# First attention: outputs kept by channel and divided by way of DMA and GpSimd, maxima turned by VectorE in 32x32 blocks

## The chip, the core and the metric

The kernel runs on one core of a Trainium2 chip, in one launch. The core has a matrix engine (TensorE, PE in the profile; its weight loads are listed apart as PEld), VectorE (DVE), ScalarE (ACT), GpSimd (POOL), and SyncE (SP), which here only issues DMAs. Each engine works through its own queue in order and waits on semaphores. The metric is the device time of one execution in microseconds (us).

## The reference

A residual stream `x` of 1024 tokens by 512 channels in float32 passes through four sublayers, each behind a LayerNorm without weights: a first attention with 32 heads of 16 channels, a feed-forward with a router and low-rank experts, a second attention with 32 heads of 128 channels, and the feed-forward again. Only the first attention and the start of the feed-forward behind it are touched here:

```python
    def attention_fwd(x, wq, wk, wv, wo, n_heads=32):
        B, T, C = x.shape
        hd = C // n_heads
        xq = (x @ wq.T).reshape(B, T, n_heads, hd)
        xk = (x @ wk.T).reshape(B, T, n_heads, hd)
        xv = (x @ wv.T).reshape(B, T, n_heads, hd)
        xq = rotary_pos_emb(xq)
        xk = rotary_pos_emb(xk)
        scale = hd ** (-0.5)
        scores = jnp.einsum('bqhd,bkhd->bhqk', xq, xk) * scale
        causal = jnp.tril(jnp.ones((T, T), dtype=bool))
        scores = jnp.where(causal[None, None], scores, NEG_INF)
        probs = jax.nn.softmax(scores.astype(jnp.float32), axis=-1).astype(xq.dtype)
        out = jnp.einsum('bhqk,bkhd->bqhd', probs, xv).reshape(B, T, C)
        return out @ wo.T
...
    x = x + _L0_attn_a_ref(_layernorm(x, axis=-1), L0_attn_a_wq, L0_attn_a_wk, L0_attn_a_wv, L0_attn_a_wo)
```

## The kernel before

**Chunks.** The 32 heads are taken four at a time, in 8 chunks `c` (`NCA`). A head has 16 channels and is padded to 32 rows (`PADA`), so a chunk fills the 128 partitions. `qT` and `kT` hold queries and keys with channels on partitions. The first padding row of each head, row `j * PADA + DA`, is one in `kT`, and in `qT` it first holds zero and later the negated maximum of each query's scores.

**Two passes of scores.** The scores of a chunk are made twice. `row_scores` (L304, matmul at L310) has queries on partitions, and `maxima` (L319, VectorE at L327 and L330) reduces them to a negated maximum per query and head, in `neg`: 128 queries on partitions, 4 heads by 4 tiles along the free side, for each half of the 1024 queries. `with_maxima` (L341) brings them into the padding row of `qT`: a transpose on TensorE (`tp_m`, L345), a copy by ScalarE (`negT`, L347) and four DMAs on SP, one per head (L350). Then `col_scores` (L355, matmul at L362) makes the scores again with keys on partitions, now with the maximum already subtracted, adds the causal mask by a matmul (L380), and `exponentials` (L382) takes their exponential.

**The product.** `product` (L384, matmul at L396) multiplies the exponentials with values into `oT`, with channels on partitions and 512 queries (`QC`) along the free side. A column of ones in the values makes the seventeenth row of each head the sum of the exponentials. ScalarE copies `oT` out of PSUM (`oTs`, L407).

**Normalization.** `normalize` (L410) turns `oTs` back to queries on partitions by four transposes on TensorE (`tp_o`, L99), copies 17 columns per head (`os`, L417), takes the reciprocal of the sums on VectorE (`rsa`, L419), and multiplies on GpSimd (L421) into `o`, which has queries on partitions and 512 channels along the free side.

**Steps.** `step(rc, cc, n)` (L440) does one of 10 steps `n` of the column work of chunk `cc` and of the row work of chunk `rc = cc + 1`, in two halves of two heads each: score matmuls of both interleaved, then maxima, exponentials, what is due, and half a product of two steps earlier. The column heads of the first half are 2 and 3. Steps 0 to 2 of the columns read the first half of the queries and steps 3 to 9 the second; the rows finish the first half of the queries within steps 0 to 2, the second in step 9. Work for later is put in `later` and run in the next step, behind the exponentials of its first half: `with_maxima(rc, 0)` in step 5, `with_maxima(cc, 1)` in step 1, the two normalizations of a chunk in step 5 and in step 2 of the next chunk.

**Order.** The code is written in an order, and a scheduler at build time follows it but lets an instruction go ahead on its engine where an earlier one isn't ready by its plan. [...]

**After the attention.** The output projection needs channels on partitions, so `gather` (L1013) transposes each tile of 128 queries again (`tp_ao`), with a copy by VectorE (`aoT`, L1016), and `out_projection` (L1019, L1022) multiplies with `wo` and adds to `x` (L1023). Two tiles are done in `tail` (L1025), with the last normalization between them; the other six in the first turns of the feed-forward (`projected`, L1042), beside its LayerNorm, whose power runs on GpSimd (L93). SP's next work is to load the weights of the second attention (L669, L671).

Of the kernel before, what the change touches and what calls it, by code (L numbers as in the profile page):

```python
# [9 lines left out]
F32 = mybir.dt.float32  # L10
BF16 = mybir.dt.bfloat16
AF = mybir.ActivationFunctionType
ALU = mybir.AluOpType
# [3 lines left out]
P = 128  # L17
T = 1024
NT = T // P
C = 512  # L20
KC = C // P
QC = 512
# [7 lines left out]
DA = C // HA  # L30
PADA = 32
# [7 lines left out]
B = 32  # L39
# [25 lines left out]
class Block:  # L65
# [174 lines left out]
    def attend_a(self, ctx_pool, pt, work, ps_s, ps_o, qT, kT, v_p, project_qk, project_v, midway, tail):  # L240
        nc, tc = self.nc, self.tc
        HC = P // PADA
        with ExitStack() as ctx:
            cp = ctx.enter_context(tc.tile_pool(name="a_c", bufs=1))
            qk = ctx.enter_context(tc.tile_pool(name="a_qk", bufs=2))
            o_sb = []

            next(project_qk)

# [26 lines left out]
            def neg(c, half):  # L276

                if (c, half) not in negs:
                    negs[c, half] = qk.tile([P, HC, NT // 2], F32, tag="neg", name=f"neg{c}_{half}", bufs=3)
                return negs[c, half]  # L280
# [59 lines left out]

            def with_maxima(c, half):  # L341

                rows = HC * NT // 2
                ps = ps_s.tile([P, QC], F32, tag="s", name=f"tp_m{c}{half}")[:rows, :P]
                nc.tensor.transpose(ps, neg(c, half).rearrange("p h i -> p (h i)"), self.ident)  # L345
                t = qk.tile([P, P], F32, tag="negT", name=f"negT{c}_{half}")[:rows, :]
                nc.scalar.copy(t, ps)  # L347
                for j in range(HC):
                    row = j * PADA + DA
                    nc.sync.dma_start(  # L350
                        qT[row : row + 1, c, half * QC : (half + 1) * QC].rearrange("o (i t) -> o i t", t=P),
                        t[j * NT // 2 : (j + 1) * NT // 2, :],
                    )

            def col_scores(c, n, heads, made):  # L355

# [27 lines left out]
            def product(c, n, p):  # L384

                first, last = n in (0, 3), n in (2, NP - 1)
                pieces = col_pieces(n)
                qc, middle = pieces[0][0], pieces[-1][-1] // 2
                if first:
                    outs[c, qc] = ps_o.tile([P, QC], F32, tag="o", name=f"oT{c}_{qc}")  # L390
                o = outs[c, qc]
                for lo, hi in ((0, middle), (middle, 2 * middle)):
                    for _, b, at, end in pieces:
                        x0, x1 = max(lo, at), min(hi, end)
                        for j in range(HC if x0 < x1 else 0):
                            nc.tensor.matmul(  # L396
                                o[rows_of(j), QC - end + x0 : QC - end + x1],
                                lhsT=v_cols(b, c * HC + j),
                                rhs=p[:, j, x0:x1],
                                start=first and x0 == 0,  # L400
                                stop=last and x1 == 2 * middle,
                            )
                    yield
                if not last:
                    return
                oT = work.tile([P, QC], F32, tag="w", name=f"oTs{c}_{qc}")
                nc.scalar.copy(oT, o)  # L407
                later.append(lambda: normalize(c, qc, oT))

            def normalize(c, qc, oT):  # L410
                if not o_sb:
                    o = ctx_pool.tile([P, NT, C], F32, tag="o", name="o")
                    o_sb.extend(o[:, i] for i in range(NT))
                ps = self.transpose4(ps_s, [oT[:, i * P : (i + 1) * P] for i in range(4)], f"o{c}{qc}", tag="s")
                pv = ps.rearrange("p a (h d) -> p a h d", d=PADA)
                os = qk.tile([P, 4, HC, DA + 1], F32, tag="os", name=f"os{c}_{qc}")
                nc.scalar.copy(os, pv[:, :, :, : DA + 1])  # L417
                rs = qk.tile([P, 4, HC], F32, tag="rs", name=f"rsa{c}_{qc}")
                nc.vector.reciprocal(rs, os[:, :, :, DA])  # L419
                for a in range(4):  # L420
                    nc.gpsimd.tensor_tensor(  # L421
                        o_sb[qc * 4 + a][:, c * HC * DA : (c + 1) * HC * DA].rearrange("p (h d) -> p h d", d=DA),
                        os[:, a, :, :DA],
                        rs[:, a, :].unsqueeze(2).to_broadcast([P, HC, DA]),
                        ALU.mult,
                    )

            def drain(gens):
                gens = list(gens)
                while gens:  # L430
                    for g in list(gens):
                        try:
                            next(g)
                        except StopIteration:
                            gens.remove(g)

            later = []
            pending = []

            def step(rc, cc, n):  # L440


                p, made, madeT = None, {}, {}
                due = list(later)
                later.clear()
                if cc is not None:
                    p = pt.tile([P, HC, QC], F32, tag="p", name=f"p{cc}_{n}")
                    pending.append((cc, n, p))
                turns = product(*pending.pop(0)) if len(pending) > 2 else iter(())
                both = rc is not None and cc is not None  # L450
                for half in range(2 if both else 1):
                    rows, cols = (2 * half, 2 * half + 1), (2 - 2 * half, 3 - 2 * half)
                    if not both:
                        rows = cols = range(HC)
                    gens = []
                    if cc is not None:
                        gens.append(col_scores(cc, n, cols, madeT))
                    if rc is not None:
                        gens.append(row_scores(rc, n, rows, made))
                    drain(gens)  # L460
                    if rc is not None:
                        maxima(rc, n, rows, made)
                    if cc is not None:
                        exponentials(n, cols, madeT, p)
                    while due:
                        due.pop(0)()
                    next(turns, None)
                drain([turns])
                if rc is not None and n == 4:
                    later.append(lambda: with_maxima(rc, 0))  # L470
                if cc is not None and n == 0:
                    later.append(lambda: with_maxima(cc, 1))


            for i in range(1, NT):
# [8 lines left out]
            for c in range(NCA):  # L484
                if c == NCA // 2:
                    midway()
                for n in range(NP):
                    step(c + 1 if c + 1 < NCA else None, c, n)
            for item in pending:
                drain([product(*item)])  # L490
            tail(o_sb, ps_s, work, later)
        return o_sb

# [490 lines left out]
def hybrid_block_kernel(  # L986
# [20 lines left out]
    nc = tc.nc  # L1007
    blk = Block(ctx, tc, x)

    ao = ctx.enter_context(tc.tile_pool(name="a_out", bufs=1))  # L1010
    wo = ao.tile([P, KC, C], F32, tag="wo", name="a_wo")

    def gather(o, i, work, tp, wtag, tag):  # L1013
        ps = blk.transpose4(tp, [o[i][:, k * P : (k + 1) * P] for k in range(KC)], f"ao{i}", tag)
        oT = work.tile([P, KC * P], F32, tag=wtag, name=f"aoT{i}").rearrange("p (k t) -> p k t", t=P)
        nc.vector.tensor_copy(oT, ps)  # L1016
        return oT

    def out_projection(i, oT, ps_m, tag):  # L1019
        pm = ps_m.tile([P, C], F32, tag=tag, name=f"pm_ao{i}")  # L1020
        for kc in range(KC):
            nc.tensor.matmul(pm, lhsT=oT[:, kc, :], rhs=wo[:, kc, :], start=(kc == 0), stop=(kc == KC - 1))  # L1022
        nc.vector.tensor_add(blk.x[i], blk.x[i], pm)  # L1023

    def tail(o, ps, work, later):  # L1025
        oTs = [gather(o, i, work, ps, "w", "s") for i in range(2)]
        out_projection(0, oTs[0], ps, "s")
        while later:
            later.pop(0)()
        out_projection(1, oTs[1], ps, "s")  # L1030

    weights = [w_baseT, w_rhT, lora_B, b_base]
    f_ctx = ExitStack()
# [8 lines left out]
    def projected(work, tp, ps_m):  # L1042
        yield
        yield
        oT = gather(o, 2, work, tp, "oT", "tp")
        for i in range(2, NT):
            nxt = gather(o, i + 1, work, tp, "oT", "tp") if i + 1 < NT else None
            out_projection(i, oT, ps_m, "pm")
            oT = nxt
            yield  # L1050

    xnT, xn = [], []
# [1 line left out]
    def normalize(i, tp):  # L1054
        if not xnT:
            xnT.append(ao.tile([P, KC, T], F32, tag="o", name="xnTb"))
            xn.append(ao.tile([P, KC, C], F32, tag="wo", name="xnb"))
        blk.normalized(i, xn[0][:, i % KC, :], "b")
        if i > 1:
            channels(i - 2, tp)  # L1060
# [77 lines left out]
```

## Time and profile before

| what | value |
|---|---|
| median of 3 runs | 1655.16 us (1654.3 to 1655.9) |
| the profiled execution's own time | 1654.29 us |
| its span on the core | 1652.2 us |
| granted TensorE clock | 1.00 |
| first attention, steps with columns | about 119 to 401 us of the span |
| `tp_o` transposes | 64 of 286 ns |
| `tp_m` transposes | 16 of 273 ns |
| `tp_ao` transposes | 32 of 276 ns |
| copies by ScalarE: `oTs`, `os`, `negT` | 16 of 592, 16 of 393, 16 of 244 ns |
| copies by VectorE: `aoT` | 8 of 686 ns |
| multiplies by GpSimd in `normalize` | 64 of 293 ns |
| DMAs of maxima on SP | 64 of 2 KB |

The page gives each engine's busy time and its share of the span. Groups of instructions are listed by line, engine and operation, with what is written and read (`out<-in`), the number of instructions, busy time and the mean of one. A line can be that of a helper: all transposes by TensorE have L99 except `tp_m`. The order of time lists start, duration, engine and line of single instructions, merged where they are alike; a bracket holds the idle time before an instruction and what ended it. For SP, the duration is the time in which the queue is held by issuing the DMA, not the time of the transfer.

### The profile page before, as it was taken

The page shows a single profiled execution, that of the slowest core. Times are in us where ns is not written, and L with a number is a line of the kernel's source. Part 1 is how long each engine was busy: PE and PEld are TensorE (multiplying, and loading weights), DVE is VectorE, ACT ScalarE, POOL GpSimd, SP SyncE. Part 2 cuts the span into 40 slices and gives each one's busy share as a digit, 9 for nine tenths or more (in the row PEclk, how much of TensorE's full clock was granted, in tenths as well). Part 3 has the DMA queues.
Part 4 walks back from the last instruction along what each step waited for, and adds up shares of the span by engine and source line. Part 5 has one row for each costly group of instructions (what it writes and reads, how often), then busy time and mean ns, then how long its engine had stood idle before and what let it go on. Part 6 is the DMA issues. An engine that isn't in the chain of part 4 may idle for free.

```text
span 1652.2 us, 31905 instructions
## 1 busy us (share of the span) xinstructions
PE 1632.8 (99%) x12920; PEld 937.4 (57%) x12920; DVE 1100.7 (67%) x2832; ACT 555.2 (34%) x1230; POOL 351.6 (21%) x524
## 2 busy tenths in 40 slices
PE   9999999999999999999999999999999999999998
PEld 5544444444654657556655765655665576556654
DVE  4557777771553886776677677677667767777762
ACT  2325565555212333233233223223323322332230
POOL 3000000001311332223213222222322222222140
PEclk9999999999999999999999999999999999999999
DMA  5000000001003200200200120020020012000001
GB/s 198 1 1 2 3 2 2 2 2 40 1 27 88 65 1 27 65 27 26 65 27 7 51 60 2 27 65 26 27 65 26 16 45 64 1 27 27 2 1 51
DMA packets 60866, 52.03 MB, mean 31 GB/s; under 512 B 5744, under 2 KB 47472, under 8 KB 60720
## 3 DMA queue, kind: packets, MB, share of 16 engines
q1 hardware_dynamic: 59408, 46.06, 9.7%
q0 software_dynamic: 784, 2.90, 0.5%
q8 instruction: 101, 1.65, 0.4%
q10 hardware_dynamic: 528, 1.05, 0.2%
q14 instruction: 45, 0.37, 0.1%
HBM read 30.98 MB, written 2.10 MB: 20 GB/s over the span
## 4 chain that ended last, share of the span: by engine, by line
PE 95%; DVE 3%; ACT 1%; POOL 1%; issue 0%; ACTq 0%; DVEq 0%; POOLq 0%
PE s L798 15%; PE pq L752 13%; PE o L842 13%; PE wo L649 12%; PE sT L362 8%; PE kv L707 7%; PE oT L396 5%; PE pm_f L606 3%; PE or L842 3%; PE s L310 2%; PE pj_v L185 2%; PE pj_q L185 2%; PE pj_k L185 2%; PE sT L380 1%; PE pm_ao L1022 1%; PE st L778 1%
## 5 line engine op out<-in xcount | busy, mean ns | idle before, releaser
L807 ACT ACTIVATE p<-p,nm 128x1024 f32<-128x1024 f32 (+7 forms) x256 | 198.2, 774 | 405.3 <-DVE nm L805 363.6
L810 POOL TENSOR_SCALAR p<-p,rs 128x1024 f32<-128x1024 f32 (+7 forms) x256 | 190.9, 747 | 644.8 <-DVE rs L809 620.9
L798 PE MATMUL s<-kT,qT 128*128 128x512 f32 (+3 forms) x768 | 296.0, 493 | 1.9 <-DVE p L800 1.8
L825 DVE STREAM_TRANSPOSE pT<-p 128x640 f32<-128x640 f32 (+4 forms) x256 | 169.0, 670 | 128.6 <-PE o L842 84.5
L752 PE MATMUL pq<-xnTb,wq 128*128 128x512 f32 x512 | 243.0, 597 | 0.0
L649 PE MATMUL wo<-wo,oT 128*128 128x512 f32 x512 | 240.7, 593 | 1.8 <-DVE nm L805 1.8
L800 DVE SCALAR_TENSOR_TENSOR p<-s,rq,rel 128x512 f32<-128x512 f32 (+3 forms) x384 | 223.9, 601 | 24.6 <-PE s L798 23.4
L798 PEld LDWEIGHTS s<-kT,qT 128*128 128x128 f32 x768 | 140.8, 190 | 164.8 <-issue 117.7
L842 PEld LDWEIGHTS o<-pT,va 32*128 32x128 f32 x5248 | 210.7, 185 | 25.5 <-issue 17.9
L842 PE MATMUL o<-pT,va 32*128 32x256 f32 (+5 forms) x5248 | 220.0, 321 | 0.0
L382 ACT ACTIVATE p<-sT 128x512 f32<-128x512 f32 (+1 forms) x320 | 159.2, 554 | 107.1 <-PE sT L380 67.6
L804 DVE TENSOR_REDUCE nm<-p 128x1 f32<-128x1024 f32 (+7 forms) x256 | 188.7, 738 | 2.9
L310 PE MATMUL s<-kT,qT 32*128 32x512 f32 (+3 forms) x768 | 169.6, 524 | 0.0
L362 PE MATMUL sT<-qT,kT 32*128 32x512 f32 (+3 forms) x768 | 160.5, 524 | 0.0
L649 PEld LDWEIGHTS wo<-wo,oT 128*128 128x128 f32 x512 | 94.6, 190 | 89.0 <-issue 76.3
L752 PEld LDWEIGHTS pq<-xnTb,wq 128*128 128x128 f32 x512 | 92.4, 190 | 88.8 <-issue 79.7
L707 PE MATMUL kv<-wkv,xnTb 128*128 128x256 f32 x512 | 116.5, 380 | 0.8 <-DVE qT L762 0.5
L707 PEld LDWEIGHTS kv<-wkv,xnTb 128*128 128x128 f32 x512 | 96.3, 190 | 20.0 <-issue 4.0
L327 DVE TENSOR_REDUCE part<-s 128x1 f32<-128x512 f32 x128 | 82.0, 685 | 36.9 <-PE s L310 31.0
L362 PEld LDWEIGHTS sT<-qT,kT 32*128 32x128 f32 x768 | 61.5, 183 | 56.3 <-issue 37.8
L396 PE MATMUL oT<-p,v_p 128*32 128x256 f32 (+1 forms) x1408 | 93.0, 350 | 0.0
L421 POOL TENSOR_TENSOR o<-os,rsa 128x64 f32<-128x64 f32 x64 | 16.7, 293 | 338.5 <-DVE rsa L419 323.4
(154 smaller groups left out, 1623.2 us busy)
## 6 DMA issues: line engine op xcount, KB each, us to landing
va<-v SPq DMA_DIRECT2D x256, 64.0 KB
wq<-in_b_WqT_dram SPq DMA_DIRECT2D x8, 1024.0 KB
wo<-in_b_WoT_dram SPq DMA_DIRECT2D x8, 1024.0 KB
x<-in_x_dram SPq DMA_DIRECT2D x8, 256.0 KB
wkv<-in_b_WkT_dram SPq DMA_DIRECT2D x8, 256.0 KB
wkv<-in_b_WvT_dram SPq DMA_DIRECT2D x8, 256.0 KB
out_dram<-x SPq DMA_DIRECT2D x8, 256.0 KB
wq<-in_a_wqT_dram ACTq DMA_DIRECT2D x1, 1024.0 KB
```

Source lines behind the costliest of these rows:

```text
L310: nc.tensor.matmul(made[j][:, at:end], lhsT=qT[rows_of(j), c, i * P : (i + 1) * P], rhs=kT[rows_of(j), c, kc * QC : kc * QC + end - at], s ...
L362: nc.tensor.matmul(made[j][:, at:end], lhsT=kT[rows_of(j), c, b * P : (b + 1) * P], rhs=qT[rows_of(j), c, (qc + 1) * QC - (end - at) : (qc ...
L396: nc.tensor.matmul(o[rows_of(j), QC - end + x0 : QC - end + x1], lhsT=v_cols(b, c * HC + j), rhs=p[:, j, x0:x1], start=first and x0 == 0, ...
L649: nc.tensor.matmul(ps, lhsT=oTs[g, h][:, t * P : (t + 1) * P], rhs=wo[:, h, :], start=(h == heads[0]), stop=(h == heads[-1]))
L707: nc.tensor.matmul(ps.rearrange("p a b -> p (a b)"), lhsT=xnT[:, kc, i * P : (i + 1) * P], rhs=wkv[:, kc].rearrange("p a b -> p (a b)"), s ...
L752: nc.tensor.matmul(ps, lhsT=wq[:, kc, hh * DB : (hh + 1) * DB], rhs=xnT[:, kc, cols], start=(kc == 0), stop=(kc == KC - 1))
L798: nc.tensor.matmul(s, lhsT=qT[:, i * P : (i + 1) * P], rhs=kT[:, lo:hi], start=True, stop=True)
L800: nc.vector.scalar_tensor_tensor(p[:, lo:hi], s, rq[:, i : i + 1], rel[:, at + lo : at + hi], ALU.mult, ALU.add)
L804: nc.vector.tensor_reduce(nm, p[:, :w], AX.X, ALU.max, negate=True)
L807: nc.scalar.activation(p[:, :w], p[:, :w], AF.Exp, bias=nm, scale=slope, accum_out=ss)
L810: nc.gpsimd.tensor_scalar(p[:, :w], p[:, :w], rs, 1.0, ALU.mult, ALU.mult)
L842: nc.tensor.matmul(cols(o[:, a], j), lhsT=vs[g][rows, j * NB + b, :], rhs=moving(j, rows, slice(b * B, (b + 1) * B)), start=(j == js[0] an ...
```

## The change

The output of the first attention stays with channels on partitions: `outs_sb` is one tile of 128 channels by 4 groups by 1024 queries. The transposes of `normalize` and `gather` and their copies are gone, and `out_projection` reads `outs_sb` directly.

The division takes another way. When a product is complete and copied to `oT` (now in a buffer of its own), eight DMAs on SP are issued at once: for each of 4 heads the row of 512 sums is spread over 32 partitions (`sums`), and the 16 rows of numerators go to their channels in `outs_sb`. `invert`, two steps later, takes the reciprocal on VectorE and issues four DMAs that gather each head's reciprocals into a row of `over`, and four that repeat this row over 16 partitions. `multiply`, four steps later, multiplies in place on GpSimd, 64 partitions by 512. `later` now holds a countdown with each entry.

The maxima are turned on VectorE, in 32x32 blocks, instead of by TensorE and ScalarE. A block transpose leaves the four blocks of 32 queries on separate groups of partitions, so each head takes four DMAs of 4 rows of 32 elements: 16 for a half in place of 4.

```diff
             def with_maxima(c, half):
 
-                rows = HC * NT // 2
-                ps = ps_s.tile([P, QC], F32, tag="s", name=f"tp_m{c}{half}")[:rows, :P]
-                nc.tensor.transpose(ps, neg(c, half).rearrange("p h i -> p (h i)"), self.ident)
-                t = qk.tile([P, P], F32, tag="negT", name=f"negT{c}_{half}")[:rows, :]
-                nc.scalar.copy(t, ps)
+                t = qk.tile([P, B], F32, tag="negT", name=f"negT{c}_{half}")
+                twice = neg(c, half).rearrange("p h i -> p (h i)").unsqueeze(1).to_broadcast([P, 2, B // 2])
+                nc.vector.transpose(t.rearrange("p (a m) -> p a m", a=2), twice)
                 for j in range(HC):
                     row = j * PADA + DA
-                    nc.sync.dma_start(
-                        qT[row : row + 1, c, half * QC : (half + 1) * QC].rearrange("o (i t) -> o i t", t=P),
-                        t[j * NT // 2 : (j + 1) * NT // 2, :],
-                    )
+                    to = qT[row : row + 1, c, half * QC : (half + 1) * QC].rearrange("o (i a t) -> o a i t", a=P // B, t=B)
+                    for a in range(P // B):
+                        m = a * B + j * NT // 2
+                        nc.sync.dma_start(to[:, a], t[m : m + NT // 2, :])
...
-                oT = work.tile([P, QC], F32, tag="w", name=f"oTs{c}_{qc}")
+                oT = qk.tile([P, QC], F32, tag="oT", name=f"oTs{c}_{qc}")
                 nc.scalar.copy(oT, o)
-                later.append(lambda: normalize(c, qc, oT))
+                normalize(c, qc, oT)
 
             def normalize(c, qc, oT):
-                if not o_sb:
-                    o = ctx_pool.tile([P, NT, C], F32, tag="o", name="o")
-                    o_sb.extend(o[:, i] for i in range(NT))
-                ps = self.transpose4(ps_s, [oT[:, i * P : (i + 1) * P] for i in range(4)], f"o{c}{qc}", tag="s")
...
+                at = c % 2 * HC * DA
+                to = outs_sb[0][at : at + HC * DA, c // 2, qc * QC : (qc + 1) * QC]
+                sums = qk.tile([P, QC // B], F32, tag="sums", name=f"sums{c}_{qc}")
+
+                over = qk.tile([P, QC], F32, tag="over", name=f"over{c}_{qc}")
+                row = P // 2 - at
+                for j in range(HC):
+                    r = j * PADA + DA
+                    nc.sync.dma_start(sums[j * B : (j + 1) * B, :], oT[r : r + 1, :].rearrange("o (x e) -> o x e", x=B))
+                for j in range(HC):
+                    nc.sync.dma_start(to[j * DA : (j + 1) * DA, :], oT[j * PADA : j * PADA + DA, :])
+
+                def invert():
+                    nc.vector.reciprocal(sums, sums)
+                    for j in range(HC):
+                        nc.sync.dma_start(
+                            over[row + j : row + j + 1, :].rearrange("o (x e) -> o x e", x=B), sums[j * B : (j + 1) * B, :]
+                        )
+                    for j in range(HC):
+                        nc.sync.dma_start(
+                            over[at + j * DA : at + (j + 1) * DA, :],
+                            over[row + j : row + j + 1, :].unsqueeze(1).to_broadcast([1, DA, QC]),
+                        )
+
+                def multiply():
+                    nc.gpsimd.tensor_tensor(to, to, over[at : at + HC * DA, :], ALU.mult)
+
+
+                later.append([1, invert])
+                later.append([3, multiply])
...
+            def due():
+
+                for x in list(later):
+                    x[0] -= 1
+                    if x[0] < 0:
+                        later.remove(x)
+                        x[1]()
...
-    def out_projection(i, oT, ps_m, tag):
+    def out_projection(oT, i, ps_m, tag):
         pm = ps_m.tile([P, C], F32, tag=tag, name=f"pm_ao{i}")
         for kc in range(KC):
-            nc.tensor.matmul(pm, lhsT=oT[:, kc, :], rhs=wo[:, kc, :], start=(kc == 0), stop=(kc == KC - 1))
+            nc.tensor.matmul(pm, lhsT=oT[:, kc, i * P : (i + 1) * P], rhs=wo[:, kc, :], start=(kc == 0), stop=(kc == KC - 1))
         nc.vector.tensor_add(blk.x[i], blk.x[i], pm)
 
-    def tail(o, ps, work, later):
-        oTs = [gather(o, i, work, ps, "w", "s") for i in range(2)]
-        out_projection(0, oTs[0], ps, "s")
+    def tail(oT, ps, later):
+        out_projection(oT, 0, ps, "s")
         while later:
-            later.pop(0)()
-        out_projection(1, oTs[1], ps, "s")
+            later.pop(0)[1]()
+        out_projection(oT, 1, ps, "s")
```

## The prediction

> **What bounds the kernel now.** I read the engine totals first, then the stage table of the first attention, then what SyncE's queue (SP) pays for one DMA, then the order of time around one hand-over of maxima.
>
> ```profile
> PE 1632.8 (99%) x12920; PEld 937.4 (57%) x12920; DVE 1100.7 (67%) x2832; ACT 555.2 (34%) x1230; POOL 351.6 (21%) x524
> ```
>
> TensorE is busy 99% of the span, so any instruction taken from it seems worth its duration. The stage table (us; then busy time of PE, PEld, DVE, ACT, POOL) says how long one chunk of heads takes:
>
> ```profile
> 155.80:192.40 36.60, 36.32 (x408) 15.76 (x402) 25.88 (x83) 21.77 (x47) 2.09 (x8) 1.00 0.01 2
> 372.30:401.30 29.00, 27.64 (x367) 13.96 (x363) 1.59 (x8) 21.20 (x48) 2.09 (x8) 1.00 0.01 2
> ```
>
> 36.6 us per chunk, 29.0 for the last, which has no row scores. SP has no column there. Its rows (min/median/max ns of an issue) are:
>
> ```profile
> L350 SPq DMA_DIRECT2D qT<-negT x64: 572/573/748, 97.7 to 381.8; - x64
> L723 SPq DMA_DIRECT2D va<-v x256: 585/599/1757, 493.8 to 1369.0; - x128
> L75 SPq DMA_DIRECT2D x<-in_x_dram x8: 328/432/640, 0.7 to 7.9; - x8
> L1075 SPq DMA_DIRECT2D out_dram<-x x8: 332/333/360, 1615.5 to 1648.9; - x8
> ```
>
> One small DMA holds SP for a third to two thirds of a microsecond. The change issues a great many of them, so this, not TensorE, decides. Two stretches of the order of time show how the maxima travel:
>
> ```profile
> 154.26 0.08 DVE L330 DVE_READ_ACCUMULATOR2_ANT neg<- 128x1 f32 x1
> 155.30 0.69 DVE L330 CUSTOM_DVE_ANT_0 junk<-s,mask 128x512 f32<-128x512 f32 x1 [0.96 <-PE s L310]
> ...
> 160.33 0.24 ACT L347 COPY negT<-tp_m 16x128 f32<-16x128 f32 x1
> ...
> 163.01 0.66 PE L99 MATMUL tp_o<-ident,oTs 128*128 128x128 f32 x4 [0.28 <-ACT oTs L407]
> ...
> 165.59 0.69 PE L362 MATMUL sT<-qT,kT 32*128 32x512 f32 x1
> ```
> ```profile
> 379.82 2.57 SPq L350 DMA_DIRECT2D qT<-negT  x4
> ...
> 382.33 2.33 PE L362 MATMUL sT<-qT,kT 32*128 32x512 f32 x8
> ...
> 383.54 0.29 PEld L362 LDWEIGHTS sT<-qT,kT 32*128 32x128 f32 x2 [0.35 <-issue]
> ```
>
> The second half's maxima of a chunk are complete at 154.34 (step 9 of the chunk before). They are turned in step 1, their DMAs start near 160.6, and step 3, the first reader, starts at 165.59. In the last chunk four DMAs take 2.57 us, 0.65 each, and the last, begun at 381.8, lets the last head go at 383.54: 1.7 us from issue to use.
>
> **Part 1, taken from TensorE.** Per chunk two sets of four transposes `tp_o` and two `tp_m`. The set at 163.01 costs 0.66 and 0.28 of waiting, 0.94. The other set with its `tp_m` costs 0.7 and the second `tp_m` 0.1, by the same order of time: 1.75 us of 36.6, leaving 34.85. ACT loses small copies and is not the bound (21.77 of 36.6).
>
> After the attention, at 401.30 to 402.75, PE does the first gathers and waits for the copy, and at 406.3 the last `tp_o`. Dropping both makes the first projection 1.45 us earlier, the chain through LayerNorm 1.6. Later, the two gathers of tiles 2 and 3 take from 411.7 to 413.2, 1.5, and four more 0.44 each. Sum of the tail: 1.6 + 1.5 + 1.8 = 4.9 us, on the path, because the feed-forward is PE back to back.
>
> **Part 2, put on SP.** A hand-over of maxima is 16 DMAs in place of 4; a normalization (two per chunk) is 4 for sums, 4 for numerators, 4 for reciprocals, 4 broadcasts, in place of none. That is 64 per chunk in place of 8.
> - Maxima: 32, each from 4 partitions like the `negT` row: 0.65 each, **20.8 us**.
> - Normalizations: 32, of 16 or 32 partitions. The nearest rows disagree: 0.33 (`out_dram`, issued alone), 0.43 (`x`, mostly back to back), 0.60 (`va`, 4 outer runs). The Trainium skill ("DMA: Bandwidth & Descriptors", section "Why a DMA increments its semaphore by 16 and not by 1") says that a transfer whose outer dimension has no factor 16 runs on fewer engines and the issuing sequencer writes the missing counts itself. The 4-run rows being the dear ones agrees with it, so I take 0.43, plus 0.08 for waits between issues (the 0.65 spacing over 0.57): 0.51, **16.3 us**. Ends: 0.38 and 0.65, 12.1 and 20.8.
>
> Sum 37.1 us per chunk, more than PE's 34.85. SP becomes the fullest queue. Since it is in order and stands at times for a copy or a reciprocal, I add 0.7 (estimate; 0 to 2): period **37.8**, 1.2 over the old one.
>
> Here a rule speaks for the change. The same page, "Issuing engines are not separate DMA queues", calls the sequencer time of starting a DMA usually small beside the DMA. By it SP would stay hidden and the whole PE gain stand: 8 x 1.75 + 4.9, about 19 us. The row says 0.57 against 1.7 from issue to use, with 64 per chunk. I go by the row.
>
> **Part 3, the longer hand-over.** From first issue to use the 16 DMAs need 15 x 0.65 + 1.7 = 11.45 us; four needed 3.65. Step 3's first half reads heads 2 and 3, the last issued. Without the transposes PE would reach step 3 at 165.59 - 1.05 = 164.5. The first half's maxima are complete after step 2 and read ten steps on; they have room. For the second half, where VectorE turns the maxima sets everything:
> - as soon as they are complete, in the 0.96 us gap before 155.30: first DMA at 154.6, use at 166.05, stall 1.5;
> - where it is written, behind the maxima of step 1's first half (end 160.54): first DMA at 160.75, use at 172.2, stall 7.7.
>
> The order within an engine isn't strictly the written one: at 407.20 VectorE did the next stage's LayerNorm statistics ahead of an earlier-written reciprocal whose input was late. VectorE has gaps here, so I take the early place. The turn itself, 128x32, lies below the 128x128 row of 0.30 us and above 0: about 0.2, hidden in the gap.
>
> **Part 4, what waits behind new waits.** The reciprocal of the sums stands in VectorE's queue ahead of maxima. When its sums are stuck on SP behind 16 maxima DMAs, the score buffers aren't freed and PE waits. Ends 0 and 2 us per chunk (two steps of lead are about 7 us); I take 0.8. The numerators are multiplied by GpSimd, 16 times at most 1.27 us (the 128x512 row of L532), instead of 64 small ones of 0.29: hidden, as POOL is busy 2 of 36.6 us. In the tail the last multiply comes after three DMA hops behind the 1.5 MB of weights issued from 401.5: I put it at about 417, and tile 4's projection needs it at about 419.5. Covered by 2.5 us. If GpSimd keeps it ahead of the LayerNorm power of tile 0, PE waits up to 7; I take 1.
>
> **The sum, against the profiled execution (1654.3 us, span 1652.2).** Chunk 0's maxima are complete in the prologue, so it only loses transposes: -0.8. Chunks 1 to 6: 6 x (1.2 + 0.8) = +12.0. Into the last chunk, 33.7 us from step 3 to step 3 become 37.8: +4.1. The last `tp_o` there: -0.9. Tail: -4.9 + 1. Total +10.5: 1664.8. The runs' median is 0.9 above the profiled execution, so **1666 us**. A measurement of this kernel tells about 0.2% (3.3 us) from no change.
>
> **Rivals.**
> - *Turned in written order* (slower): part 3's second case. 7 x (7.7 - 1.75) + 2.1 for the last chunk (first DMA at 374.2, use at 385.65 in place of 383.54) - 0.9 - 4.9 + 1 = +39: **1694**. For it: `negT` was copied where it is written; against: the reordering at 407.
> - *SP dearer* (slower): new DMAs like the `va` row, 0.65: SP 41.6 + 0.7 = 42.3, 6 x (5.7 + 0.8) + 8.6 - 5.6 = +42: **1697**. For it: both are SBUF to SBUF; against: its 4 outer runs.
> - *SP keeps pace* (faster): 0.38 each gives SP 32.9, below PE's 34.85, and only the stall of 1.5 stays: 6 x (1.5 - 1.75) - 0.8 + 2.1 - 0.9 - 4.9 = -6: **1649**. It decides as soon as the 32 new DMAs cost under 0.44 on average and no reciprocal blocks VectorE. For it: the 0.33 row; against: that row is of DMAs issued alone.
> - *Issue hidden altogether*, the rule's case (faster): -19, **1636**. Against it: 0.573 in nearly each of 64 cases.
>
> **How the numbers follow.** Forecast 0.42 (its own range 1655 to 1680); written order 0.22; SP dearer 0.18; SP keeps pace 0.11; issue hidden 0.04; a feedback of late DMAs into buffers, above 1702, 0.03. Faster are the fourth and fifth: 0.15. Of the forecast 0.08 lies within 0.2%. The rest, 0.77, is slower. The range 1645 to 1702 leaves out the hidden case, the feedback, and the ends of the others.
>
> **What would show it.** SP's issues in the attention: 512 in place of 64, a median of 0.57 for maxima and about 0.43 for the others; chunk periods near 38 us in the stage table; PE waiting for `sT` at step 3 of a chunk, released by DMA; VectorE turning maxima about 6 us ahead of step 1's end (right) or behind its maxima (the first rival). No PE gap there and periods under 35.5 would prove the forecast wrong.

## The result, and the profile after

The changed kernel takes **1736.28 us** (1733.94 to 1737.88) where the kernel before takes 1655.15 on the same chip: a ratio of 1.0489, 95% interval 1.0471 to 1.0507. The forecast was 1666 with a range of 1645 to 1702. The sign was right, the size was not: +81 us came where +10.5 were summed. The profiled execution took 1733.94 us, with a span of 1732.2.

The page of the kernel after, its engine totals and two rows of its 40 slices:

```profile
PE 1650.5 (95%) x12808; PEld 935.5 (54%) x12808; DVE 1095.6 (63%) x2840; ACT 549.0 (32%) x1198; POOL 355.6 (21%) x476
...
PE   9999777777999999999999999999999999999998
...
PEclk9999888889899999999999999999999999999999
```

TensorE has 112 instructions fewer and is busy 18 us longer. Slices 5 to 10, within the attention's steps, hold idle time (each of them was a 9 for TensorE before), and the granted clock is lower in slices 5 to 9 and 11. The slices behind are full, as before.

The stage table, first for one chunk, then for that chunk cut at its gap (columns as before: stretch, us, busy PE, PEld, DVE, ACT, POOL, granted clock, DMA share, GB/s):

```profile
355.08:402.95 47.87, 38.72 (x394) 15.81 (x392) 25.83 (x85) 21.04 (x42) 2.52 (x2) 0.89 0.19 13
...
376.10:384.80 8.70, 0.05 (x4) 0.00 (x0) 0.82 (x3) 0.50 (x2) 1.25 (x1) 0.68 0.05 8
384.80:400.30 15.50, 15.46 (x148) 6.57 (x148) 11.34 (x38) 6.85 (x14) 1.27 (x1) 0.85 0.27 15
```

A chunk takes 47.87 us where it took 36.6 (37.8 were forecast). For 8.7 us of it every engine but SP is almost idle. The waits, summed over 100 to 500 us (engine and tile, what ended the wait, us in total, times, longest), one row from VectorE's list and one from TensorE's:

```profile
DVE sums L426 <- DMA sums<-oTs: 116.7, 15, 14.0
```
```profile
PE sT L360 <- DVE part L327: 56.6, 13, 8.7
```

TensorE waits for VectorE, and VectorE waits at the reciprocal (L426) for its sums. The chain of waits through the same gap gives the order in which each step released the next:

```profile
379.50 0.57 SPq L351
380.18 0.58 SPq L421
380.80 0.58 SPq L421
381.42 0.59 SPq L421
382.06 1.74 DMA sums<-oTs
383.98 0.25 DVE sums L426
384.24 0.55 DVE part L327
384.83 1.22 PE sT L360
```

SP issues maxima until 380.1. Only then can it issue the sums of a product that ScalarE had copied by 372.0. They land at 383.8, the reciprocal of 0.25 us runs, VectorE frees a score buffer with the next reduction, and TensorE starts again. VectorE's own order of time shows the turn of the maxima and the two reciprocals of the chunk:

```profile
352.13 0.21 DVE L345 STREAM_TRANSPOSE negT<-neg 128x32 f32<-128x32 f32 x1
...
366.37 0.25 DVE L426 RECIPROCAL sums<-sums 128x16 f32<-128x16 f32 x1 [3.37 <-DMA sums<-oTs]
...
383.98 0.25 DVE L426 RECIPROCAL sums<-sums 128x16 f32<-128x16 f32 x1 [10.84 <-DMA sums<-oTs]
```

The maxima are turned at once, in the gap ahead of the next maxima: the early place that was forecast. The reciprocals wait 3.37 and 10.84 us, 14.2 per chunk. The second one was moved at build time four reductions ahead of its written place (it stands behind 10 of the chunk's 16, and behind 14 in experiment 5, which holds it in its place), so those four wait behind it. SP's order of time over the same stretch (start, duration, a row for each run of equal DMAs):

```profile
352.42 10.12 SPq L351 DMA_DIRECT2D qT<-negT  x16
362.64 2.46 SPq L421 DMA_DIRECT2D sums<-oTs  x4
365.14 2.48 SPq L423 DMA_DIRECT2D o<-oTs  x4
367.74 2.42 SPq L428 DMA_DIRECT2D over<-sums  x4
370.26 2.78 SPq L432 DMA_DIRECT2D over<-over  x4
373.10 6.98 SPq L351 DMA_DIRECT2D qT<-negT  x11
380.18 2.47 SPq L421 DMA_DIRECT2D sums<-oTs  x4
382.69 2.48 SPq L423 DMA_DIRECT2D o<-oTs  x4
385.22 3.19 SPq L351 DMA_DIRECT2D qT<-negT  x5
388.52 2.42 SPq L428 DMA_DIRECT2D over<-sums  x4
391.04 2.45 SPq L432 DMA_DIRECT2D over<-over  x4
```

Two things are to be seen. SP works without a pause from 352.4 to 393.5, 41.1 us for 64 DMAs. And the 11 maxima from 373.10 are those of the next chunk's first half, which nobody reads before that chunk's step 0, at about 399.8, yet they stand ahead of the sums for which VectorE waits. The price of one issue (min/median/max ns):

```profile
L351 SPq DMA_DIRECT2D qT<-negT x256: 572/573/744, 83.8 to 457.5; - x128
...
L421 SPq DMA_DIRECT2D sums<-oTs x64: 517/588/1357, 140.1 to 483.0; - x64
L423 SPq DMA_DIRECT2D o<-oTs x64: 535/588/1371, 142.7 to 485.6; - x64
L428 SPq DMA_DIRECT2D over<-sums x64: 508/588/1022, 145.7 to 490.8; - x64
L432 SPq DMA_DIRECT2D over<-over x64: 507/539/1475, 148.2 to 493.3; - x64
```

The new DMAs cost 0.54 to 0.59 us (medians), not the 0.43 that was taken.

**The chunk's account.** +8.7 for the gap; +2.3 for the clock (below); about +1.0 for step 3, whose first score block takes 2.1 us in place of 1.1 while maxima arrive; about +0.6 for step 4, whose first block takes 1.64 in place of 1.07 behind the first late reciprocal; +0.2 of small gaps (0.45 in all, where 0.28 were); about -1.4 for the transposes (1.13 for those of the outputs, by experiment 8, and about 0.3 for `tp_m`, by experiment 2). That is +11.4, against 47.9 - 36.6 = 11.3; the small terms are read off the order of time. The clock: TensorE's order of time behind the gap has

```profile
384.83 1.22 PE L360 MATMUL sT<-qT,kT 32*128 32x512 f32 x1 [8.68 <-DVE part L327]
...
388.45 1.17 PE L310 MATMUL s<-kT,qT 32*128 32x512 f32 x1
...
389.46 0.59 PE L360 MATMUL sT<-qT,kT 32*128 32x512 f32 x1
```

The same matmul takes 1.2 us until 389.46, and half of that from there. In the stage table a granted clock of 0.85 over 15.5 us is 0.15 x 15.5 / 0.5 = 4.65 us at half clock, at whose end 2.3 us of work are missing. The Trainium skill ("TensorE: Matmul & The Clock Gate", Part 1: The HAM clock gate) says that after an idle activity window of about 3.4 us the array gets every second pulse, until it has been busy again for as long. The trace agrees that the clock is halved, but not in both lengths: the 0.68 of the gap is 5.6 us at half clock, so it began about 3.1 us into the 8.7, and the recovery took 4.65 us of work.

**After the attention.** From the attention's end (478.9; 401.3 before) to the end of the span are 1253.3 us, where there were 1250.9: 2.4 lost, 3.9 gained in the forecast. Only 0.5 of the 2.4 stands at the first matmul of the second attention (562.8; 484.7 before). 1.5 come from 1638.5 to 1700.6, in code that the change leaves alone, where the granted clock is 0.97 in place of 1.00. TensorE and GpSimd behind the attention:

```profile
478.92 2.84 PE L1039 MATMUL pm_ao<-a_wo,o 128*128 128x512 f32 x6
483.86 1.26 POOL L438 TENSOR_TENSOR o<-o,over 64x512 f32<-64x512 f32 x1 [10.12 <-DMA over<-over]
485.17 6.16 PE L1039 MATMUL pm_ao<-a_wo,o 128*128 128x512 f32 x10 [3.41 <-POOL o L438]
```

Six matmuls of the first two projections run, and then the multiply of the last chunk's first half isn't there. It had not been priced; only the second half's was. The clock is halved here too: these ten matmuls take 6.16 us, where eight take 3.60 later.

### The profile page after: what moved, and what is told of

It reads as the page before. It is cut to its first block, busy times and chain, and to the rows that moved or that the text cites. A ratio compares the mean times of both kernels' runs of the same rounds, so it can differ in the third digit from the quotient of the medians.

```text
span 1732.2 us, 32242 instructions
## 1 busy us (share of the span) xinstructions
PE 1650.5 (95%) x12808; PEld 935.5 (54%) x12808; DVE 1095.6 (63%) x2840; ACT 549.0 (32%) x1198; POOL 355.6 (21%) x476
## 4 chain that ended last, share of the span: by engine, by line
PE 87%; SPq 4%; DVE 3%; DMA 3%; ACT 2%; POOL 1%; issue 1%; DVEq 0%; ACTq 0%; POOLq 0%
PE s L821 14%; PE pq L775 13%; PE o L865 12%; PE wo L672 12%; PE sT L360 7%; PE kv L730 6%; PE oT L394 3%; PE pm_f L629 3%; PE or L865 3%; PE s L310 2%; PE pj_v L185 2%; PE pj_q L185 2%; PE pj_k L185 2%; DMA sums<-oTs 2%; SPq L421 1%; SPq L351 1%
## 5 line engine op out<-in xcount | busy, mean ns | idle before, releaser
L360 PE MATMUL sT<-qT,kT 32*128 32x512 f32 (+3 forms) x768 | 185.4, 558 | 58.7 <-DVE part L327 56.6
L310 PE MATMUL s<-kT,qT 32*128 32x512 f32 (+3 forms) x768 | 191.2, 553 | 0.0
L360 PEld LDWEIGHTS sT<-qT,kT 32*128 32x128 f32 x768 | 68.5, 194 | 126.4 <-DVE part L327 71.6
L438 POOL TENSOR_TENSOR o<-o,over 64x512 f32<-64x512 f32 x16 | 20.2, 1264 | 411.8 <-DMA over<-over 232.8
L394 PE MATMUL oT<-p,v_p 128*32 128x256 f32 (+1 forms) x1408 | 96.6, 363 | 3.3 <-ACT oTs L405 3.3
```

The lines of the kernel that those rows point to most:

```text
L310: nc.tensor.matmul(made[j][:, at:end], lhsT=qT[rows_of(j), c, i * P : (i + 1) * P], rhs=kT[rows_of(j), c, kc * QC : kc * QC + end - at], s ...
L360: nc.tensor.matmul(made[j][:, at:end], lhsT=kT[rows_of(j), c, b * P : (b + 1) * P], rhs=qT[rows_of(j), c, (qc + 1) * QC - (end - at) : (qc ...
```

## The experiments

Two explanations stood against each other. By the first, the loss is VectorE's wait at the reciprocal, with the halved clock behind it. By the second, it is SP's load of 64 DMAs per chunk, whoever waits for it. All times are medians, beside 1654.6 to 1655.3 for the kernel before.

**1. The normalization alone**: the changed kernel with the maxima by TensorE and four DMAs, as before.

```diff
-                nc.vector.transpose(t.rearrange("p (a m) -> p a m", a=2), twice)
+                nc.tensor.transpose(ps, neg(c, half).rearrange("p h i -> p (h i)"), self.ident)
...
+                nc.scalar.copy(t, ps)
```

> The change with the maxima turned as before (TensorE, ScalarE, 4 DMAs a half). Theory A (VectorE stands at the reciprocal of the sums because their DMAs wait on SP behind 16 maxima DMAs): SP then has 8 x 0.66 + 32 x 0.62 = 25 us of issues in a chunk of about 35, the sums go out at once, VectorE's wait for them falls from 14 us a chunk to under 2, no PE gap and no halved clock: 1640 to 1660. Theory B (the detour of the division itself, three DMA hops and GpSimd, is what PE waits for): nearly all of the loss stays, above 1710. Theory C (SP's total of issues sets the period): like A, no longer full, about 1645.

Measured: 1679.96 us, ratio 1.0150 (1.0133 to 1.0167). Slower than 1640 to 1660, though SP has 40 DMAs per chunk, some 25 us of 41. VectorE's waits tell why:

```profile
DVE sums L428 <- DMA sums<-oTs: 38.5, 10, 12.2
...
DVE sums L428 <- DMA o<-oTs: 27.8, 5, 10.8
```

Both rows are waits of the reciprocal, together 66 us in place of 117. TensorE's gaps are 1 to 3 us and the chunk takes about 41. So a queue that isn't full still brings the sums late. An estimate from the trace of the change says why: sums issued at once, at 372.0, would land at about 372.0 + 2.5 + 1.7 = 376.2, and VectorE stood at its moved reciprocal from 373.1.

**2. The maxima alone**: the kernel before with VectorE's turn and 16 DMAs per half.

```diff
-                nc.tensor.transpose(ps, neg(c, half).rearrange("p h i -> p (h i)"), self.ident)
...
+                nc.vector.transpose(t.rearrange("p (a m) -> p a m", a=2), twice)
```

> The kernel before with the maxima turned by VectorE and sent by 16 DMAs a half; normalization and gathers as before. A: SP has 32 x 0.65 = 21 us of issues a chunk and nothing else; VectorE waits for no DMA; the hand-over of the second half ends 1 to 2 us late at step 3, less 0.3 for the transposes gone: 8 chunks x 1 = 1660 to 1668. Theory D (the longer hand-over of maxima is the main cost): above 1710.

Measured: 1660.30 us, 1.0033 (1.0019 to 1.0046). From the third chunk on a chunk takes 36.56 us, 0.05 less than before: dropping `tp_m` gains about 0.3, and step 3 gives most of it back, as its first block takes 1.35 us (240.86 to 242.21) in place of 1.07. So 32 maxima DMAs alone cost nothing there. The loss lies at the two ends. By the third chunk TensorE is 2.2 us behind the kernel before (a product at 207.29 in place of 205.12), and it still is in the last (380.12 in place of 377.90). There step 3 has no row scores beside it and loses 2.0 more: its scores run from 384.1 to 388.9, with a wait for `qT<-negT` of 1.44 us among them.

**3. The reciprocal off VectorE**: as a power of -1 on GpSimd.

```diff
-                    nc.vector.reciprocal(sums, sums)
+                    nc.gpsimd.tensor_tensor(sums, sums, minus1, ALU.pow)
```

> The change with one instruction moved: the reciprocal of the sums is a power of -1 on GpSimd instead of VectorE. All 64 DMAs a chunk stay. A: maxima no longer stand behind a DMA wait, the PE gap of 8.7 us and the halved clock behind it go; what is left is SP's 64 x 0.64 = 41 us a chunk against 47.8: 1736 - 7 x 6.5 = about 1690, between 1675 and 1700. C (SP's issues alone set the period, the wait of VectorE is where it shows): the wait moves elsewhere, above 1720.

Measured: 1705.32 us, 1.0306 (1.0291 to 1.0321). 31 us of the 81 go with VectorE's wait, 50 stay. GpSimd now does the waiting, the power takes 2.9 us where VectorE needs 0.25, and TensorE's first wait is for the maxima's DMAs:

```profile
PE sT L362 <- DMA qT<-negT: 19.6, 14, 2.5
```

Neither explanation is enough alone.

**4. The normalization's DMAs on GpSimd's queue.**

```diff
-                    nc.sync.dma_start(sums[j * B : (j + 1) * B, :], oT[r : r + 1, :].rearrange("o (x e) -> o x e", x=B))
+                    nc.gpsimd.dma_start(sums[j * B : (j + 1) * B, :], oT[r : r + 1, :].rearrange("o (x e) -> o x e", x=B))
```

and so for the other three kinds.

> The change with the 16 DMAs of each normalization issued by GpSimd's queue; SP keeps the 32 of maxima a chunk (21 us). A and C: sums no longer wait behind maxima, VectorE waits 2 to 3 us at most per reciprocal, GpSimd has 32 issues of 0.55 to 1 us, 18 to 32 us of a chunk: 1650 to 1680. B: above 1710, since the hops of the division stay as long.

Measured: 1699.14 us, 1.0268 (1.0252 to 1.0283), above what was expected. The reason is in the order of time on GpSimd and then on VectorE:

```profile
310.31 1.25 POOL L438 TENSOR_TENSOR o<-o,over 64x512 f32<-64x512 f32 x1 [4.46 <-DMA over<-over]
311.52 2.03 POOL L421 DMA_DIRECT2D sums<-oTs  x4
```
```profile
314.64 0.25 DVE L426 RECIPROCAL sums<-sums 128x16 f32<-128x16 f32 x1 [8.07 <-DMA sums<-oTs]
```

GpSimd stands 4.46 us at the multiply of one normalization, and behind it stands the issue of the next one's sums, for which VectorE stands in turn. The block had only changed queues.

**5 and 6. The reciprocal in its written place, then later.** The first keeps the build from moving it forward; the second also gives its countdown three steps in place of one and the multiply six in place of three (the last chunk keeps 1 and 3).

```diff
-                    nc.vector.reciprocal(sums, sums)
+                    tc.keep_in_program_order(nc.vector.reciprocal(sums, sums))
...
-                later.append([1, invert])
-                later.append([3, multiply])
+                later.append([3 if c < NCA - 1 else 1, invert])
+                later.append([6 if c < NCA - 1 else 3, multiply])
```

> The change with one word added: the reciprocal of the sums is held to its written place in VectorE's order, where the build had moved it ahead by one to four maxima; countdowns as they are. A (VectorE stands at a reciprocal whose sums are late): the second reciprocal of a chunk waited 10.8 us; its written place is some 3 to 4 us later in the maxima, so it waits about 7 less what SP gains: 1705 to 1725. C (SP's issues alone set the period): no difference, above 1730.

> Like e5, and reciprocal and multiply are due 4 and 7 steps behind the product in place of 2 and 4 (not in the last chunk). A: by then the sums have landed, VectorE waits for no DMA in chunks 0 to 6, and as in the run with the reciprocal on GpSimd only SP's queue is left, 41 to 44 us a chunk: 1690 to 1712. B (the division's detour is what PE waits for): longer still than the change, above 1740.

Measured: 1722.86 us, 1.0408 (1.0393 to 1.0424), for the place alone, and 1704.50, 1.0297 (1.0281 to 1.0312), for both. Kept in order, the gaps shrink from 8.4 to about 6.3 us. With the later countdown VectorE doesn't wait at the reciprocal before the last chunk, and TensorE waits for something else:

```profile
PE sT L360 <- DMA qT<-negT: 23.8, 15, 5.5
```

The chunks still take 43 to 45 us. This is the second explanation, bare: SP needs 41, and the maxima come at the end of what it has queued.

**7. SP's load without its results**: experiment 2, with the 16 DMAs of each normalization added into tiles that nothing reads; the division itself stays as before, on TensorE.

```diff
                 later.append(lambda: normalize(c, qc, oT))
+                copies(c, qc, oT)
```

> SP's load by itself: maxima by VectorE with 16 DMAs a half, normalization and gathers as before (transposes, old reciprocal), and besides the 16 DMAs of each new normalization copied into spare tiles that nobody reads. No engine but SP waits for them. C: SP has 64 x 0.64 = 41 us a chunk, 42 to 44 with its own waits, and hands the maxima over that late: 1690 to 1710. A alone (only the reciprocal's wait matters): SP's load is hidden, 1660 to 1670 as with the maxima alone.

Measured: 1705.38 us, 1.0306 (1.0289 to 1.0323), 45 more than experiment 2. TensorE does all its old transposes of outputs here, and no engine waits for a new result; only SP's queue is as full as in the change. A chunk takes about 45 us, as TensorE waits for the maxima once in each of six chunks, and the clock is halved behind each wait:

```profile
PE sT L360 <- DMA qT<-negT: 28.9, 6, 5.2
```

**8. Both causes away**: experiment 1 (eight maxima DMAs per chunk) with the order and the countdowns of experiment 6.

> The late reciprocal, and the maxima turned as before by TensorE with 4 DMAs a half: SP has 25 us of issues a chunk. A and C: no VectorE wait and no full queue in the chunks, PE back to back at 36.6 - 1.6 = 35 us a chunk; the end of the attention and the first projections stay as long as in e1 (about 12 us lost there against 5 gained): 1640 to 1655. If a wait of VectorE for DMAs stays, about 1670.

Measured: 1654.84 us, 0.9996 (0.9987 to 1.0004). Together with the others this makes a square:

| us | reciprocal as built, 1 and 3 steps | in order, 3 and 6 steps |
|---|---|---|
| 32 maxima DMAs per chunk | 1736.28 | 1704.50 |
| 8 maxima DMAs per chunk | 1679.96 | 1654.84 |

The reciprocal's place is worth 32 us with SP full and 25 with SP light; the turn by VectorE with its 24 further DMAs is worth 56 and 50, and experiment 7 shows that a full queue costs about as much (45) when nobody reads its results. The two causes are nearly additive, and with both away the time is that of the kernel before. Not run: all 64 DMAs on SP with only their order changed, the sums ahead of maxima that aren't needed yet. The stage table for one chunk, from product to product, in the kernel before and in experiment 8, and TensorE at the beginning of the second:

```profile
199.62:236.23 36.61, 36.34 (x402) 15.76 (x402) 25.88 (x83) 21.77 (x47) 2.09 (x8) 1.00 0.01 2
```
```profile
198.06:233.54 35.48, 35.20 (x395) 14.92 (x395) 25.75 (x83) 21.10 (x45) 2.54 (x2) 1.00 0.25 18
```
```profile
198.06 0.64 PE L396 MATMUL oT<-p,v_p 128*32 128x256 f32 x8 [0.27 <-ACT oTs L407]
```

With no wait for a DMA in it the chunk takes 35.48 in place of 36.61, a gain of 1.13, and the clock is 1.00. The 0.27 is the wait for the copy that stood ahead of `tp_o` before: the next product needs the same PSUM buffer, so it stayed when the transposes went. The attention ends at 393.3 in place of 401.3. That the time as a whole is unchanged comes from TensorE's wait behind it, and from the half clock behind that:

```profile
PE pm_ao L1041 <- POOL o L440: 8.9, 1, 8.9
```
```profile
405.11 7.42 PE L1041 MATMUL pm_ao<-a_wo,o 128*128 128x512 f32 x10 [8.95 <-POOL o L440]
```

**9 and 10. The end.** Experiment 8 with the DMAs of the last chunk's first half on GpSimd's queue, and the same with both halves of the last chunk there.

```diff
+                q = nc.gpsimd if c == NCA - 1 and qc == 0 else nc.sync
...
-                    nc.sync.dma_start(sums[j * B : (j + 1) * B, :], oT[r : r + 1, :].rearrange("o (x e) -> o x e", x=B))
+                    q.dma_start(sums[j * B : (j + 1) * B, :], oT[r : r + 1, :].rearrange("o (x e) -> o x e", x=B))
```

and so for the other three kinds.

> As the kernel with the maxima on TensorE, the reciprocal kept in place and the countdowns 3 and 6, but the 16 DMAs of one normalization, the last chunk's first half, are issued by GpSimd. Theory: the chunks were already 1.6 us shorter each, and the gain was given back because the first projection waited for this one normalization in SP's queue; on another queue the wait of 8.9 us ahead of it and most of its 19.2 us go, and the time falls to 1638 to 1648 us. Rival (the wait at the end is made by what the multiplication itself stands behind on GpSimd, not by SP's queue): 1652 to 1657, no change.

> The same, with both normalizations of the last chunk issued by GpSimd. Theory: 1638 to 1648 us as with the first half alone, since the second half is needed four projections later; if GpSimd's queue then holds up the LayerNorm powers that stand behind it, up to 5 us more than the run with one half. Rival: 1652 to 1657.

Measured: **1647.60 us** (1646.6 to 1648.59), 0.9951 (0.9937 to 0.9964), and 1648.14, 0.9953 (0.9941 to 0.9966). Both are about 0.5% faster than the kernel before, clear of its noise, and not told apart from each other. In the first, TensorE's order of time has

```profile
393.77 2.84 PE L1042 MATMUL pm_ao<-a_wo,o 128*128 128x512 f32 x6
399.54 6.09 PE L1042 MATMUL pm_ao<-a_wo,o 128*128 128x512 f32 x10 [2.92 <-POOL o L441]
```

The wait is 2.92 us in place of 8.95, and the ten matmuls behind it take 6.09 in place of 7.42: together 7.4 us less, and the time fell by 7.2. No run takes away what is left (eight of these matmuls take 3.60 at full clock).

## Why the prediction was right or wrong

**The bound was named rightly**: SP's issue, not TensorE's work. Experiment 7 shows it alone: 45 us from DMAs whose results nobody reads. The rule that was weighed, that starting a DMA is usually small beside the DMA, would have given 1636; here one issue is 0.54 to 0.59 us, against 1.74 from the end of the last issue to the landing in the chain above, and 64 of them take 41.1 us, more than a chunk of 36.6. But two terms of the sum failed: the price of SP in Part 2 and the wait of VectorE in Part 4.

**Part 1** took 1.75 us per chunk from TensorE. Measured: 1.13 for the outputs (experiment 8) and about 0.3 for the maxima (experiment 2), about 1.4. The 0.28 of waiting counted with `tp_o` moved to the next product.

**Part 2, the first step that failed, by size**: "I take 0.43, plus 0.08 for waits between issues". The new DMAs took 0.54 to 0.59, and with the spaces about 0.63. The upper end, 0.65, was nearest, and so was the rival *SP dearer*: SP 41.1 us where it said 41.6 and the forecast 37.1. Its transfers have outer runs of 16 or 32 and cost as much as those with 4, so the split by outer runs that chose 0.43 doesn't show here. The 0.7 added for SP's own pauses was small too. The rival priced a full SP at 1697; experiments 6 and 7, where it acts without the reciprocal, give 1704.5 and 1705.4, which by itself lies outside the range of 1645 to 1702. In experiment 7 SP pauses for the copies of the products, about 3 us per chunk: the maxima come last in its queue, and their lateness delays the products whose sums it sends next. In experiment 6 it also stands, 12.4 us in all, for the gathers of the reciprocals to land.

**Part 3** was right in its mechanism. The maxima are turned in the early place, in 0.21 us (0.2 estimated), and the hand-over stalls about 1 us (1.5). The maxima of the first half, though, are read eight steps after step 2, not ten. And the sign that was named, TensorE waiting at step 3 for a DMA, is the smaller one: 2.1 us in all, against 56.6 for VectorE.

**Part 4, the second step that failed**: "Ends 0 and 2 us per chunk; I take 0.8", argued from two steps of lead being about 7 us. The wait was named, and its size was wrong: VectorE stands 14.2 us per chunk, TensorE 8.7 of them, and the clock takes 2.3 more. Three things were missed. The two steps count from the copy of the product, but SP comes to its sums 8.2 us after that (380.18 against 372.0), as the next hand-over, which isn't needed before the next chunk, stands ahead. The build moved the reciprocal further forward; the prediction used that reordering for the maxima and didn't ask what it does to the reciprocal. And a gap of this length costs the clock behind it, which the sum put at nothing. By experiments 5 and 6 this step is 32 of the 81 us; the rest goes with SP's load.

**The tail** was to gain 3.9 us. By the start of the second attention it had lost 0.5. The projections that follow do come faster, 4.8 us apart in place of 5.24. But the first two need the first half's multiply of the last chunk, whose chain the sum had left out. Experiment 9 shows that SP's queue made most of that wait in experiment 8; in the changed kernel itself this was not tried.

## What to carry to other kernels

Price a queue of small DMAs by its own issue row before anything else, and compare the sum with the period of the stage: here 25 us of issue per chunk could be hidden (experiment 8) and 41 could not (experiments 6 and 7). Then ask of each instruction that waits for such a DMA what stands ahead of it in that queue and what stands behind it on its own engine; put it where its data has long arrived, and hold it there, since a build may move it forward. At the end of a stage, follow the last item separately: nothing is left there to hide its chain of hops.

## What the runs showed of the hardware

- In the gap of 8.7 us TensorE's clock halved about 3.1 us in and stayed so for 4.65 us of work behind it. The length of a gap alone doesn't tell: in experiment 1 a gap of 2.28 us was followed by 6.8 us at about half clock (0.52 from 344.0 to 350.8) and gaps of up to 1.6 us by none, and in experiment 4 a gap of 3.90 us passed at full clock, which then halved about 0.6 us into the work behind it (the same matmul takes 0.69 at 269.38 and 1.22 at 272.75). With no gap (experiment 8) it is 1.00 in the chunk.
- GpSimd issues one of these DMAs in 0.49 to 0.50 us, SP in 0.54 to 0.59, so a change of queue alone makes an issue little cheaper.
- A power on GpSimd over 128x16 takes 2.9 us, VectorE's reciprocal 0.25, and VectorE's block transpose of 128x32 takes 0.21.
